# GpSimd's add of the diagonal's first tile, one step later

## The chip, the cores and the metric

The kernel runs on one core of one Trainium2 chip. The metric is the device time of one execution in microseconds (us). The kernel before takes 2315.55 us, the median of 3 runs (2315.52 to 2318.34).

The engines' names in the profile: PE is the matrix engine TensorE (PEld its weight loads), DVE is VectorE, ACT is ScalarE, POOL is GpSimd, SP is SyncE, which issues most of the transfers.

## What is computed

A transformer block with adaptive layer norm, in float32. x has 2 batches of 2048 tokens with 512 features; there are 16 heads of 32 features, and the MLP's hidden width is 2048:

```python
mod = silu(condition) @ Wada + bada
sh_a, sc_a, gt_a, sh_m, sc_m, gt_m = split(mod, 6, axis=1)
xm = layernorm(x, g1, be1) * (1 + sc_a) + sh_a
# attention(xm): q, k, v from xm @ Wqkv
scores = q k^T * hd**-0.5;  scores = where(causal, scores, -inf)
out = (softmax(scores) v) @ Wproj + bproj
x = x + gt_a * out
xm = layernorm(x, g2, be2) * (1 + sc_m) + sh_m
x = x + gt_m * (gelu(xm @ W1 + b1) @ W2 + b2)
```

## The kernel before

The work goes in phases: queries, keys and values of the first batch (with the weight preparation beside it), attention of the first batch, its output projection, the same three for the second batch, and then the two layers of the MLP for both batches. The change lies in the attention phase.

**Units and steps.** Attention of a batch is 16 units (c, i): a chunk c of four heads, and a block i of 512 queries (i from 0 to 3). The first chunk takes the blocks in the order 0, 1, 2, 3, the others in the order 0, 2, 1, 3. So units 3, 7, 11 and 15 have i = 3, and units 6, 10 and 14 have i = 1. A unit walks over the keys up to its queries in 4i + 3 steps (`steps_of`, line 696). The first 4i steps have one full tile of 128 keys each, all of it below the diagonal. The last three are the diagonal: step 4i has its first tile (d0 in what follows), step 4i + 1 has the second and the fourth tile packed together (d1), and step 4i + 2 the third (d2).

**What a step does.** `scores_t` (line 594) computes the transposed scores of the step's keys for four heads into PSUM (`st`: a product `fold` x `sel` that subtracts each row's maximum, and one of keys and queries). ScalarE writes the exponentials into the tile `e` (line 635), of which there are four slots (`E_BUFS`). On the diagonal GpSimd then sets what lies above it to zero with `affine_select` (line 643): one instruction for d0, two for d1, one for d2. Two steps later (`LAG`) TensorE multiplies the masked tile by the values into `o`.

**The softmax's sums.** For the full steps and for d0 the exponential tiles are added up before they are summed over the keys: the first two of a group of four tiles start a chain `ee` (`begin_chain`, line 664), the others are added (`add_to`, line 661, both through `add`, line 654). One add is a GpSimd instruction of 128 x 2048 elements (line 656). In the last unit of a batch it is four VectorE instructions of 128 x 512 (line 659). A product `sm<-ee` with a matrix of ones then sums the chain over its keys. d0's tile goes into the unit's last chain, whose product comes four steps after d0. d1 and d2 are summed by products of their own (`sm<-e`). There are two slots of `ee`.

**Scores ahead.** Between these products TensorE also computes scores of later units (`s`), whose row maxima VectorE takes (lines 495 and 500). How many are put into a step follows from costs (`due`, `weight`).

**What sets the order.** Matmuls, and the instructions that are wrapped in `act(...)`, keep the order in which the program issues them, each on its engine. This holds for the exponentials, the masks and the adds. A planner places the rest, transfers among them, by its own model of the time, so their order can change with a change elsewhere. GpSimd carries masks and adds in one stream, in program order.

**Around the end of the attention.** In the last unit `prepare` (line 446) multiplies the first attention outputs by the softmax's inverses on VectorE (line 467) and adds a bias row on GpSimd (line 465). `finish` (line 676) stores a unit's output and sums (lines 684 and 683). The output projection (`project_phase`, line 1209) loads the sums' last part (`r`, line 373), rows of x (`xt`, line 1225) and two attention outputs (`at`, line 1234), and multiplies `at` on GpSimd (line 1265) before TensorE multiplies it by the projection weights (`ps_o`). In the first batch weight pieces of the MLP are loaded in the same stretch (line 1153) into slots of `qst` and `vv`.

Of the kernel before, what the change touches and what calls it, by code (L numbers as in the profile page):

```python
# [27 lines left out]
def dit_block_kernel(  # L28
# [43 lines left out]
    TQ = QB // P  # L72
# [512 lines left out]
    def attention_phase(row):  # L585
        b, vv, kst, qst = row.b, row.vv, row.kst, row.qst
        with pool(f"att{b}") as ap, pool(
# [66 lines left out]
            def add(u, dst, x, y):  # L654
                if u < len(units) - 1:
                    act(nc.gpsimd.tensor_tensor(dst, x, y, ALU.add))  # L656
                    return
                for h in range(HC):
                    act(nc.vector.tensor_tensor(dst[:, h], x[:, h], y[:, h], ALU.add))

            def add_to(u, chain, es):
                add(u, chain, chain, es)

            def begin_chain(u, es0, es1):
                chain = ap.tile([P, HC, QB], F32, tag="ee", name="ee", bufs=EE_BUFS)
                add(u, chain, es0, es1)
                return chain

            def products(dst, lhs, es, q0, at, first, last):
                for h in range(HC):  # L670
                    mm(
                        dst[h * HD : (h + 1) * HD, q0:], lhs(h),
                        es[:, h, at : at + QB - q0], start=first, stop=last,
                    )

            def finish(u, o, sm):

                c, i = units[u]
                ot = ap.tile([P, QB], F32, tag="ot", name="ot", bufs=2)
                act(nc.scalar.copy(ot, o))  # L680
                sums = ap.tile([P, QB], F32, tag="sums", name="sums", bufs=2)
                act(nc.scalar.copy(sums, sm))
                nc.sync.dma_start(sums_d[b][u], sums[0:P:HD, :])
                nc.sync.dma_start(od[b][i][:, c, :], ot)
# [5 lines left out]
            def flush(upto):  # L690
                while pending and pending[0][0] <= upto:
                    pending.pop(0)[1]()
# [16 lines left out]
            def due(u, step):  # L709

                rate, past = 0.0, weight[step]
                for v in range(u + 1, len(units)):

                    left = sum(weight[step : max(step + 1, starts[v] - 3)])
                    rate = max(rate, (cum[v] - row.spent) / left)
                return row.spent + rate * past

            for u, (c, i) in enumerate(units):
                if NQ <= u + AHEAD < len(units):
                    row.load_queries(u + AHEAD)  # L720
                if u % NQ == 0 and c + 1 < C:
                    row.load_keys(c + 1, 0, NG)
                steps = len(steps_of[u])
                for n_step, tiles in enumerate(steps_of[u]):
                    last = n_step == steps - 1
                    if n_step == 0:
                        summed = set()
                        o = ps_op.tile([P, QB], F32, tag="o", name="o")
                        sm = ps_op.tile([P, QB], F32, tag="sm", name="sm")
                    ready = row.at  # L730

                    n = row.count(
                        due(u, starts[u] + n_step) - QB // 2,
                        u + AHEAD - (n_step < 2 and u > 0),
                    )
                    if u == 0 and n_step < LAG:

                        n = max(n, HC)
                    es, rest = scores_t(u, n_step, n)
                    rest = len(row.todo) - rest  # L740
                    make_rows = False
                    if u + 1 < len(units) and row.rows_made == u + 1:
                        if last:
                            row.score(row.count(cum[-1], u + 1))
                        make_rows = last or (ready > u + 1 and n_step >= 1)
                    row.inverses(u, n_step)
                    if u == len(units) - 1:
                        row.prepare(n_step)
                    if make_rows and not last:
                        row.rows(u + 1)  # L750
                    flush(now)
                    if make_rows and last:
                        row.rows(u + 1)
                    row.score(max(0, len(row.todo) - rest))

                    def tile_by_tile(dst, lhs, es, tiles, first, last):
                        at = 0
                        for n, (j, q) in enumerate(tiles):
                            products(
                                dst, lambda h: lhs(j, h), es, q, at,  # L760
                                first and n == 0, last and n == len(tiles) - 1,
                            )
                            at += QB - q

                    def values(es=es, tiles=tiles, c=c, o=o, first=n_step == 0, last=last):
                        tile_by_tile(
                            o,
                            lambda j, h: vv[:, j, (c * HC + h) * HD : (c * HC + h + 1) * HD],
                            es, tiles, first, last,
                        )  # L770

                    def row_sums(es, last, tiles=((0, 0),), sm=sm, summed=summed):
                        first = not summed
                        summed.add(len(summed))
                        tile_by_tile(sm, lambda j, h: ones[:, :HD], es, tiles, first, last)

                    pending.append((now + LAG, values))
                    sums_of, wait = None, 0
                    if n_step < i * TQ:
                        k = n_step % TQ  # L780
                        if k == 0:
                            even = es
                        elif k == 1:
                            chain = begin_chain(u, even, es)
                        else:
                            add_to(u, chain, es)
                        if k == TQ - 1 and n_step + 1 < i * TQ:
                            sums_of, wait = (chain, False), 2
                    elif i and n_step == i * TQ:
                        add_to(u, chain, es)  # L790
                        sums_of, wait = (chain, False), 2
                    else:

                        sums_of, wait = (es, last, tiles), i > 0 and not last
                    if sums_of:
                        pending.append(
                            (now + LAG + wait, lambda f=row_sums, s=sums_of: f(*s))
                        )
                    if last:
                        pending.append((now + LAG, lambda u=u, o=o, sm=sm: finish(u, o, sm)))  # L800
                    pending.sort(key=lambda p: p[0])
                    now += 1
# [471 lines left out]
    with pool("wada") as wp, pool("qkv0") as qp, pool("hl0") as hp, pool(  # L1274
# [161 lines left out]
        pieces.done()  # L1436

    attention_phase(row)


    past, row = row, Row(1)
    with pool("qkv1") as qp, pool("ps_qkv1", bufs=6, space=PSUM) as ps_mm:
# [29 lines left out]
        with pool("hl1") as hp:  # L1472
# [17 lines left out]
            pieces.done()  # L1490

    attention_phase(row)
    ps_s_cm.__exit__(None, None, None)

# [541 lines left out]
```

## Time and profile before

| what | us |
|---|---|
| median of 3 runs | 2315.55 |
| the profiled execution | 2314.76 |
| its span, first to last instruction | 2313.0 |
| TensorE busy in the span | 2252.9 (97%) |
| GpSimd busy in the span | 1021.5 (44%) |
| ScalarE busy in the span | 1006.2 (44%) |
| attention, first batch | from about 212 to 736 |
| attention, second batch | from about 973 to 1494 |
| one GpSimd add (line 656), mean | 4.58 |
| one GpSimd mask (line 643), median | 0.637 |

A row of the timeline is: start in us, length in us, engine, line, operation, the tile written and the tiles read, the shape, how many instructions are merged, and in brackets how long the engine was idle before it and what ended that wait. A row of the waits is: who waited, for whom, the sum in us, how often, the longest. A row by stretch has the window, its length, the busy time and count of each engine, then TensorE's granted clock (1.00 is full speed), the share of the transfer engines and GB/s. Idle time of an engine that is not the bottleneck costs nothing.

### The profile page before, as it was taken

What the parts mean: (1) busy time and instruction counts of PE and PEld (TensorE: products, weight loads), DVE (VectorE), ACT (ScalarE), POOL (GpSimd) and SP (SyncE); (2) the same over time, 40 slices, a digit from 0 to 9 for tenths busy, and PEclk for the clock granted to TensorE, in tenths of its full rate; (3) what the DMA queues carried; (4) which work ended last, traced back from release to release, by engine and by line L of the source; (5) the groups of instructions that cost most, each with busy time, mean ns of one, the idle gap of its engine ahead of it and who ended that gap; (6) DMA issues with size and microseconds to landing.
All of it is one profiled execution on the core that took longest, in us unless ns stands there. A gap on an engine that the chain in (4) does not pass through costs nothing.

```text
span 2313.0 us, 32545 instructions
## 1 busy us (share of the span) xinstructions
PE 2252.9 (97%) x12033; PEld 1374.5 (59%) x12033; DVE 1443.8 (62%) x3025; ACT 1006.2 (44%) x1952; POOL 1021.5 (44%) x561
## 2 busy tenths in 40 slices
PE   7999999999999999999999999999999999999998
PEld 5777555555544588755555554344684585486477
DVE  4677766767757667777577766662573483375366
ACT  4434555555555244355555556513313322332320
POOL 7252986877782692278777879340000000000000
PEclk9999999999999999999999999999999999999999
DMA  9877143231323796523223123272354253353433
GB/s 302 279 259 195 37 92 69 65 83 47 99 94 128 258 300 230 162 67 78 71 72 88 47 74 114 98 254 86 118 165 150 99 174 130 116 171 121 153 113 131
DMA packets 160505, 311.52 MB, mean 135 GB/s; under 512 B 16545, under 2 KB 48845, under 8 KB 158553
## 3 DMA queue, kind: packets, MB, share of 16 engines
q1 hardware_dynamic: 155488, 285.53, 40.9%
q0 software_dynamic: 4480, 23.36, 2.6%
q8 instruction: 95, 1.56, 0.3%
q14 instruction: 66, 0.53, 0.1%
q10 hardware_dynamic: 376, 0.55, 0.1%
HBM read 229.95 MB, written 87.29 MB: 137 GB/s over the span
## 4 chain that ended last, share of the span: by engine, by line
PE 84%; POOL 6%; DVE 5%; issue 2%; ACT 1%; DMA 1%; SPq 0%; POOLq 0%; DVEq 0%; ACTq 0%
PE ps_a L206 24%; PE st L206 16%; PE ps_b L206 12%; PE o L206 9%; PE s L206 8%; PE ps_c L206 6%; POOL ee L656 4%; PE sm L206 4%; PE ps_o L206 2%; DVE junk L495 2%; PE ps_xt L214 1%; DVE mx L500 1%; ACT e L635 1%; PE ps_o L214 1%; POOL e L643 0%
## 5 line engine op out<-in xcount | busy, mean ns | idle before, releaser
L635 ACT ACTIVATE e<-st 128x512 f32<-128x512 f32 (+1 forms) x1152 | 571.5, 578 | 392.9 <-PE st L206 370.6
L500 DVE TENSOR_REDUCE mx<-s 128x1 f32<-128x512 f32 x578 | 381.6, 686 | 223.0 <-PE s L206 221.9
L656 POOL TENSOR_TENSOR ee<-ee,e 128x2048 f32<-128x2048 f32 x106 | 485.8, 4583 | 16.3 <-ACT e L635 9.0
L206 PE MATMUL st<-qst,kst 128*128 128x512 f32 (+3 forms) x1280 | 412.4, 388 | 0.0
L206 PE MATMUL s<-kst,qst 128*128 128x512 f32 (+3 forms) x1054 | 381.2, 393 | 10.7 <-DVE mx L500 6.1
L206 PE MATMUL ps_a<-sum,w 128*128 128x256 f32 (+1 forms) x1088 | 346.6, 454 | 0.0
L206 PE MATMUL o<-e,vv 128*32 128x512 f32 (+3 forms) x2560 | 293.7, 540 | 9.4 <-POOL e L643 9.3
L206 PEld LDWEIGHTS st<-qst,kst 128*128 128x128 f32 x1280 | 230.0, 189 | 100.6 <-issue 67.6
L206 PEld LDWEIGHTS ps_a<-sum,w 128*128 128x128 f32 x1088 | 206.3, 190 | 109.8 <-issue 91.4
L495 DVE CUSTOM_DVE_ANT_0 junk<-s,causal 128x128 bf16<-128x128 f32 (+3 forms) x476 | 224.9, 472 | 65.0 <-PE s L206 51.3
L656 POOL TENSOR_TENSOR ee<-e 128x2048 f32<-128x2048 f32 x42 | 192.5, 4583 | 138.9 <-ACT e L635 130.8
L206 PEld LDWEIGHTS s<-kst,qst 128*128 128x128 f32 x1054 | 196.0, 188 | 70.5 <-DVE mx L500 21.7
L1615 DVE TENSOR_TENSOR h<-c,ps_b 128x512 f32<-128x512 f32 x32 | 22.0, 688 | 202.4 <-PE ps_b L206 202.4
L206 PEld LDWEIGHTS <-sel 32*128 32x128 bf16 x1152 | 29.4, 91 | 196.2 <-issue 196.2
L500 DVE TENSOR_REDUCE mx<-st 128x1 f32<-128x512 f32 x190 | 129.6, 682 | 0.4
L643 POOL TENSOR_SCALAR_AFFINE_SELECT e<-e 128x512 f32<-128x512 f32 x128 | 82.1, 663 | 91.8 <-ACT e L635 89.6
L1789 ACT ACTIVATE h<-h,cols 128x512 f32<-128x512 f32 x96 | 69.3, 722 | 120.4 <-DVE h L1615 120.4
L206 PE MATMUL ps_b<-sum,w 128*128 128x256 f32 (+1 forms) x384 | 120.6, 450 | 0.0
L206 PE MATMUL st<-fold,sel 32*128 32x512 bf16 (+1 forms) x1152 | 117.5, 374 | 2.8 <-DVE mx L495 1.7
L206 PEld LDWEIGHTS o<-e,vv 128*32 128x32 f32 x2560 | 57.8, 109 | 96.2 <-issue 64.3
L984 POOL TENSOR_TENSOR lo<-lo,hi 128x512 fp32r<-128x512 f32 x32 | 40.8, 1276 | 132.4 <-ACT hi L982 130.7
L206 PEld LDWEIGHTS ps_b<-sum,w 128*128 128x128 f32 x384 | 73.0, 190 | 37.2 <-issue 30.6
(206 smaller groups left out, 3094.7 us busy)
## 6 DMA issues: line engine op xcount, KB each, us to landing
kst<-k SPq DMA_DIRECT2D x128, 256.0 KB
qst<-q SPq DMA_DIRECT2D x128, 256.0 KB
w<-w1d SPq DMA_DIRECT2D x32, 896.0 KB
w<-w2d SPq DMA_DIRECT2D x28, 1024.0 KB
w<-w2d SPq DMA_DIRECT2D x28, 768.0 KB
q<-hi SPq DMA_DIRECT2D x32, 256.0 KB
q<-lo SPq DMA_DIRECT2D x32, 256.0 KB
k<-hi SPq DMA_DIRECT2D x32, 256.0 KB
```

The costliest lines, as they stand in the source:

```text
L206: return tc.keep_in_program_order(nc.tensor.matmul(*args, **kw))
L214: return tc.keep_in_program_order(nc.tensor.transpose(dst, src, ident[:n, :n]))
L495: nc.vector.tensor_tensor_reduce(junk[:, :w], x, causal[:, QB - w :], 1.0, MASKED, ALU.add, ALU.max, m,)
L500: nc.vector.tensor_reduce(m, x, axis=AX.X, op=ALU.max)
L635: act(nc.scalar.activation(e4[:, h, :w], sts[h][:, :w], AF.Exp))
L643: nc.gpsimd.affine_select(d, d, pattern=[[0, HC], [1, P]], compare_op=ALU.is_ge, fill=0.0, base=0, channel_multiplier=-1,)
L656: act(nc.gpsimd.tensor_tensor(dst, x, y, ALU.add))
L984: engine.tensor_tensor(lo, d, hi.bitcast(F32), ALU.subtract)
L1615: act(nc.vector.tensor_tensor(dst, x, y, ALU.add))
L1789: nc.scalar.activation(d, ps, AF.Gelu, bias=col(r_b1 + half * HF + f, 1))
```

## The change

In units with i > 0 the add of d0's tile to the chain is not issued in d0's step any more. The tile is kept under the name `single`, and the add is issued in the next step, after `scores_t` has issued the exponentials and the two masks of d1. The step at which the product `sm<-ee` is issued stays the same. Units with i = 0 have no chain and are untouched. In the last unit of each batch the same move holds for VectorE's four adds.

```diff
                     pending.append((now + LAG, values))
                     sums_of, wait = None, 0
+                    if i and n_step == i * TQ + 1:
+                        add_to(u, chain, single)
                     if n_step < i * TQ:
                         k = n_step % TQ
                         if k == 0:
...
                         if k == TQ - 1 and n_step + 1 < i * TQ:
                             sums_of, wait = (chain, False), 2
                     elif i and n_step == i * TQ:
-                        add_to(u, chain, es)
+                        single = es
                         sums_of, wait = (chain, False), 2
                     else:
```

## The prediction

> **What bounds the kernel now.** I read the page's busy line first, then the table by stretch of the span, then the list of waits with TensorE as the waiter, and last the order of time around each wait.
>
> ```profile
> span 2313.0 us, 32545 instructions
> PE 2252.9 (97%) x12033; PEld 1374.5 (59%) x12033; DVE 1443.8 (62%) x3025; ACT 1006.2 (44%) x1952; POOL 1021.5 (44%) x561
> ...
> 212.00:736.00 524.00, 513.04 (x3661) 264.64 (x3661) 364.49 (x886) 302.36 (x608) 385.04 (x142) 0.99 0.31 78
> ...
> 973.00:1494.00 521.00, 510.29 (x3661) 263.29 (x3660) 364.54 (x886) 302.39 (x608) 385.20 (x142) 1.00 0.30 78
> 1494.00:1560.00 66.00, 66.00 (x185) 31.55 (x184) 40.36 (x73) 9.22 (x15) 30.43 (x25) 1.00 0.75 254
> ...
> PE o L206 <- POOL e L643: 9.3, 8, 2.4
> ```
>
> TensorE is the bound: busy 97%. The stretches 212 to 736 and 973 to 1494 are the two attention phases. In them TensorE stands idle about 11 us each, and the only wait on GpSimd there is the value product `o` waiting for a causal mask: 9.3 us in 8 waits. The changed line touches exactly these masks. GpSimd works in order, so the 4.6 us add of the first diagonal tile (d0) stands in front of the masks of the second diagonal step (d1). A unit with much work behind shows the chain (GpSimd, ScalarE and TensorE in order of time, unit 14 of the first batch):
>
> ```profile
> 682.08 0.63 POOL L643 TENSOR_SCALAR_AFFINE_SELECT e<-e 128x512 f32<-128x512 f32 x1
> 682.80 4.56 POOL L656 TENSOR_TENSOR ee<-ee,e 128x2048 f32<-128x2048 f32 x1
> 687.29 1.84 POOL L643 TENSOR_SCALAR_AFFINE_SELECT e<-e 128x512 f32<-128x512 f32 x3
> ...
> 680.07 2.06 ACT L635 ACTIVATE e<-st 128x512 f32<-128x512 f32 x4 [0.95 <-PE st L206]
> ...
> 688.00 1.93 PE L206 MATMUL o<-e,vv 128*32 128x384 f32 x16 [2.43 <-POOL e L643]
> 692.42 1.94 PE L206 MATMUL sm<-ee,ones 128*32 128x512 f32 x8
> 696.12 0.40 PE L206 MATMUL st<-fold,sel 32*128 32x512 bf16 x4
> ...
> 688.00:694.00 6.00, 6.00 (x32) 2.27 (x36) 2.04 (x4) 2.07 (x4) 1.12 (x2) 0.50 0.01 2
> ```
>
> The exponentials of d1 end at 682.13, but their masks start at 687.29, when the add is through, and the product of d1 waits 2.43 us. The last line is a stretch (TensorE, weight loads, DVE, ACT, POOL busy, then the granted clock): right behind the wait the clock is 0.50. So a wait is paid twice here, once as idle time and once as slow matmuls. The other units with such a wait:
>
> ```profile
> 345.92 1.64 PE L206 MATMUL o<-e,vv 128*32 128x384 f32 x16 [1.90 <-POOL e L643]
> 350.15 1.06 PE L206 MATMUL sm<-ee,ones 128*32 128x512 f32 x8
> ...
> 1106.75 1.07 PE L206 MATMUL o<-e,vv 128*32 128x384 f32 x16 [1.63 <-POOL e L643]
> 1109.44 1.06 PE L206 MATMUL sm<-ee,ones 128*32 128x512 f32 x8
> ...
> 1443.64 1.20 PE L206 MATMUL st<-qst,kst 128*128 128x512 f32 x4
> 1447.27 1.07 PE L206 MATMUL o<-e,vv 128*32 128x384 f32 x16 [2.43 <-POOL e L643]
> 1448.28 0.39 PE L206 MATMUL st<-fold,sel 32*128 32x512 bf16 x4
> 1454.03 0.39 PE L206 MATMUL st<-fold,sel 32*128 32x512 bf16 x4
> ```
>
> **The change part by part.** No instruction is added or removed. 22 GpSimd adds (11 units of each batch) go from in front of the two masks of d1 to behind them; in the last unit of each batch the four VectorE adds go behind one multiplication of line 467. In the order in which the changed kernel is built, TensorE and ScalarE keep their order exactly.
>
> *The idle time removed.* Four waits: 1.90 + 2.43 + 1.63 + 2.43 = 8.4 us. (What is left of the 9.3 lies in the two last units, whose adds are VectorE's; it stays.) In unit 14 the masks of d1 can start at 682.7, when the mask of d0 ends, and are done at 684.0, 1.6 us ahead of the product's turn at 685.57 (688.00 - 2.43).
>
> *The slow clock removed.* The two units 3 do the same matmuls from `o` to `sm`: 350.15 - 345.92 = 4.23 us against 1109.44 - 1106.75 = 2.69, so the slow clock cost the first 1.54. In unit 14 of the first batch 6.0 us ran at 0.50, so 3.0 us were lost. From `o` to the second next `st<-fold` it took 696.12 - 688.00 = 8.12 us there and 1454.03 - 1447.27 = 6.76 in the second batch: the second lost 3.0 - 1.36 = 1.6. Sum 1.5 + 3.0 + 1.6 = 6.1 us, if without the wait the clock stays up.
> A rule bears on this. The Trainium skill, "TensorE: Matmul & The Clock Gate", section "Why this matters for your kernels", says that throughput falls in mid-kernel when TensorE idles longer than about 3 us between bursts. By it gaps of 1.90 and 2.43 us would leave the clock alone, the slow stretches would have another cause and stay, and the sum would lose these 6.1 us. The trace does not agree (0.50 right behind the 2.43 us wait, and full speed behind the 1.63 us one), so I take the rows.
>
> *What the later add makes late.* Its readers are the row-sum product `sm<-ee`, the slot of `e` that the exponential four steps on wants, and the mask of the third diagonal step (d2) behind it. In unit 14 the add would run from 684.0 to 688.6 (4.56). TensorE, no longer held, reaches `sm<-ee` after `o` (1.01 = 1448.28 - 1447.27), the `st<-fold` group (0.39) and four `st` (1.20), the last two overlapping 0.07 each: 685.57 + 2.46 = 688.0. A new wait of 0.6 us, twice: 1.2 us. The mask of d2 then ends at 689.2, ahead of its product. In units without a backlog GpSimd idles until the exponentials of d1 are there, the worst case for the add's end:
>
> ```profile
> 284.07 4.58 POOL L656 TENSOR_TENSOR ee<-ee,e 128x2048 f32<-128x2048 f32 x1
> 283.73 2.07 ACT L635 ACTIVATE e<-st 128x512 f32<-128x512 f32 x4 [1.73 <-PE st L206]
> 294.00 2.06 ACT L635 ACTIVATE e<-st 128x512 f32<-128x512 f32 x4 [1.40 <-PE st L206]
> 295.65 1.06 PE L206 MATMUL sm<-ee,ones 128*32 128x512 f32 x8
> ```
>
> There the add starts at 285.80 + 1.3 (two masks) = 287.1 and ends at 291.7, before the slot is wanted (294.00) and the sum is read (295.65). It costs nothing as long as these 2.3 us of cover last. The VectorE adds of the last units end within about half a us of where they did, under a wait of `o` for a mask that exists already: nothing.
>
> *SyncE's queue, which the planner reorders.* At the end of the first batch the built order puts three of the four `qst` weight loads (line 1153 before) ahead of the stores of `ot` and `sums`, and three `vv` weight loads ahead of the load of `r`. Before:
>
> ```profile
> 735.96 0.32 SPq L684 DMA_DIRECT2D o<-ot  x1
> 736.44 0.52 SPq L683 DMA_DIRECT2D sum<-sums  x1
> 741.11 1.92 SPq L1153 DMA_DIRECT2D qst<-in_L_cond_W_dram  x4
> 743.12 0.41 SPq L373 DMA_DIRECT2D r<-sum  x1
> ...
> 746.42 0.43 SPq L1234 DMA_DIRECT2D at<-o  x1
> ...
> SPq L1153 <- POOL kst L1265: 4.1, 1, 4.1
> ...
> 755.14 1.27 POOL L1265 TENSOR_TENSOR at<-at,qst 128x512 f32<-128x512 f32 x1 [7.17 <-DMA at<-o]
> 765.50 1.27 POOL L1265 TENSOR_TENSOR at<-at,qst 128x512 f32<-128x512 f32 x1
> ...
> 735.56 20.87 PE L206 MATMUL ps_o<-kst 128*128 128x512 f32 x48
> ...
> 764.01 3.94 PE L206 MATMUL ps_o<-kst,at 128*128 128x512 f32 x8
> ...
> 768.66 24.20 PE L206 MATMUL ps_o<-kst,at 128*128 128x512 f32 x56
> ...
> DMA packets 3660, 7.58 MB, mean 303 GB/s; under 512 B 602, under 2 KB 1626, under 8 KB 3276
> ...
> qst<-in_L_cond_W_dram SPq DMA_DIRECT2D x4, 128.0 KB
> ```
>
> SyncE is held at the `qst` loads until 741.11, for GpSimd's multiplications of line 1265 (the wait of 4.1 us). After the change both stores and three more loads are issued behind that point: 0.48 + 0.52 + 3 x 0.48 = 2.4 us more before `at` is issued at 746.42. By data it is the same: 256 KB of `ot` and 3 x 128 KB more ahead of `at` at 303 GB/s is 2.1 us. `at` landed at 755.1 and its last part was multiplied at 766.77; TensorE wanted it one pair before the end of its first eight (764.01 + 6 x 20.87 / 48 = 766.6). So there is no cover: TensorE waits 2.4 us more, a gap as long as those of unit 14, so I add one slow stretch of 1.6 us (as in unit 14 of the second batch). Bounds: nothing (the load comes no later, because transfers overlap) and 2.4 + 3.0 = 5.4 us. I take 4.0, nearest to the rows of unit 14. In the second batch only stores and weight loads trade places, and TensorE is busy without a gap from 1494 to 1560; I take nothing.
>
> *Sum.* -8.4 - 6.1 + 1.2 + 4.0 = -9.3 us. The profiled execution took 2314.76 us (span 2313.0), so 2305.5; the median of the runs is 0.8 above it. I predict 2306 us.
>
> **The rivals.**
> - The stores and loads at the batch's end are hidden after all: -13.3 us, 2302. For it: transfers overlap, and the issue of `x` loads behind also gets easier. Against it: the load of `at` is waited for 7.17 us by GpSimd already.
> - The slow clock is not the waits' doing (the skill's rule above gives this too, by itself): -8.4 + 1.2 + 2.4 = -4.8, 2311. Against it: in the attention I find the clock low only right behind such waits.
> - The wait only moves: the row sums or the slot of `e` hold TensorE as long as the masks did. This needs the add to end about 2 us later than worked out in the units with a backlog. Then 8.4 is paid elsewhere and 4.0 is added: about 2315 to 2319.
> - Slower, by one thing: the late `at`. If TensorE comes out of that wait slow and stays slow, the output projection, 24.2 us of work behind 768.66, drags. It decides once more than 13.3 - 2.4 = 10.9 us of that work run at 0.50; all of it would give 13 us more than before, 2329. Against it: the slow stretches above lost 1.5 to 3.0 us each and ended by themselves.
>
> **How the numbers follow.** Likeliest (2306) 0.57, hidden at the batch's end 0.22, clock independent 0.08, wait moves 0.08, projection drags 0.05. A measurement here tells about 0.2% (4.6 us) from no change, so faster means under 2310.9. The likeliest and the hidden case lie there almost wholly, of the third half: faster 0.81; the third's other half and much of the fourth within 0.2%: 0.11; slower 0.08. The range goes from 2300 (hidden, and the new 1.2 us waits gone too) to 2312 (the clock case and a transition at its upper bound).
>
> **What would show it.** The waits of `o` on the mask should be gone except in the last units (under 1 us in all). The granted clock should be 1.0 through both attention phases, with no 0.50 stretch behind units 3 and 14. `sm<-ee` should wait on line 656's add for about 0.6 us in the two units 14. SyncE should issue `at` about 2.4 us later after the last product of the first batch, and TensorE show a gap of some 3 us in the first `ps_o<-kst,at` group, perhaps a 0.50 clock behind it. I am wrong if other diagonal steps show new waits, or if the clock falls in the attention without a wait before it.

## The result and the profile after

The changed kernel takes 2307.71 us, the median of 7 runs (2305.5 to 2309.61). The kernel before, run on the same chip, takes 2315.52 us (7 runs, 2310.09 to 2319.1). The ratio is 0.9966, with a 95% interval from 0.9952 to 0.998: 7.8 us less. The profiled execution is the fastest of the seven, 2305.5 us with a span of 2303.7, against 2314.76 and 2313.0 before.

Of the kernel after, the first two lines of the page (span; busy time of each engine, share and instructions):

```profile
span 2303.7 us, 32538 instructions
...
PE 2250.5 (98%) x12033; PEld 1374.2 (60%) x12033; DVE 1439.6 (62%) x3025; ACT 1006.1 (44%) x1952; POOL 1021.1 (44%) x561
```

The work is the same. TensorE is busy 2.4 us less (2252.9 to 2250.5) and idle 6.9 us less (60.1 to 53.2): a part of the gain are matmuls that ran faster. The two profiles also differ in a slow stretch outside the attention: in the kernel after the clock is 0.50 from 890.28 to 893.69 us, behind a wait of 2.52 us ahead of the second batch's attention, and in the kernel before it is 1.00 behind the same wait. Of the kernel after, TensorE's waits (waiter, whom it waited for, sum, how often, longest):

```profile
PE sm L206 <- DVE ee L659: 1.3, 2, 0.6
PE ps_o L206 <- POOL at L1267: 1.1, 1, 1.1
...
PE sm L206 <- POOL ee L656: 0.8, 2, 0.4
...
PE o L206 <- POOL e L643: 0.2, 1, 0.2
```

The wait of `o` on the masks has shrunk from 9.3 us in 8 to 0.2 us. In its place stand the two predicted waits of the row sums on the add (0.8 us), one at the batch's end (1.1 us), and one of the last units, `sm` on VectorE's adds (1.3 us), which I had not predicted. Of the kernel after, GpSimd, TensorE and the stretch behind in unit 14 of the first batch (rows as those of the unit in the prediction):

```profile
679.16 1.81 POOL L643 TENSOR_SCALAR_AFFINE_SELECT e<-e 128x512 f32<-128x512 f32 x3
680.93 4.56 POOL L656 TENSOR_TENSOR ee<-ee,e 128x2048 f32<-128x2048 f32 x1
685.45 0.64 POOL L643 TENSOR_SCALAR_AFFINE_SELECT e<-e 128x512 f32<-128x512 f32 x1
...
682.61 1.07 PE L206 MATMUL o<-e,vv 128*32 128x384 f32 x16
...
685.55 1.07 PE L206 MATMUL sm<-ee,ones 128*32 128x512 f32 x8 [0.42 <-POOL ee L656]
...
685.50:691.00 5.50, 5.45 (x60) 2.19 (x60) 3.67 (x6) 4.94 (x10) 0.58 (x1) 1.00 0.14 51
```

The three masks of d0 and d1 now run as one group (x3) ahead of the add and end at 680.97. The product of d1 starts at 682.61 without a wait, and takes 1.07 us where it took 1.93. The sum waits 0.42 us for the add, and the clock behind is 1.00.

To see where the time went I measured each unit from its first `o` product to that of the next one (for the last unit: to the first `ps_o`; for the projection: from there to the first `ps_a`). Units that are not in the table agree within 0.1 us, but for unit 6 of the second batch (+0.34).

| stretch (us) | before | after | difference |
|---|---|---|---|
| unit 3, batch 1 / 2 | 53.70 / 52.14 | 50.80 / 51.06 | -2.91 / -1.08 |
| unit 13, batch 1 / 2 | 39.21 / 39.24 | 39.10 / 39.10 | -0.11 / -0.14 |
| unit 14, batch 1 / 2 | 25.70 / 24.31 | 20.75 / 20.75 | -4.95 / -3.56 |
| unit 15, batch 1 / 2 | 37.99 / 37.99 | 39.20 / 39.19 | +1.21 / +1.20 |
| projection, batch 1 | 57.13 | 58.13 | +1.00 |

Units 3, 13 and 14 gain 12.8 us, and the last units and the projection give 3.4 back. That leaves -9.3; the small rest (+0.1) makes it the -9.26 between the two profiled executions.

### The profile page after: what moved, and what is told of

Same layout as the page of the kernel before. It is cut to its first block, busy times and chain, and to the rows that moved or that the text cites. A ratio compares the mean times of both kernels' runs of the same rounds, so it can differ in the third digit from the quotient of the medians.

```text
span 2303.7 us, 32538 instructions
## 1 busy us (share of the span) xinstructions
PE 2250.5 (98%) x12033; PEld 1374.2 (60%) x12033; DVE 1439.6 (62%) x3025; ACT 1006.1 (44%) x1952; POOL 1021.1 (44%) x561
```

## The experiments

Two questions stood open. Where do the 3.4 us given back come from? And is the slow clock really the waits' doing? Every kernel below computes the whole block. Differences are against runs of the kernel before on the same chip; `units` in the diffs has 16 entries, so `len(units) - 1` is the last unit, whose adds are VectorE's.

**GpSimd's adds alone** (`pool_only`). The add moves in all units but the last.

```diff
+                    if i and n_step == i * TQ + 1 and u < len(units) - 1:
+                        add_to(u, chain, single)
...
-                        add_to(u, chain, es)
+                        single = es
+                        if not (u < len(units) - 1):
+                            add_to(u, chain, es)
```

> The add moves in the units whose adds are GpSimd's; the last unit of each batch keeps VectorE's adds where they were, and SyncE's order is then the one of before. My theory: the change's gain is all in units 3 and 14 (wait plus slow clock, -2.9, -1.1, -5.0 and -3.6 us by the trace of the change), and the last unit's part only costs (1.2 us in each batch, and 1.0 in the first projection). So this is faster than the change by about 3.4 us: ratio to before about 0.995, some 2304 us; the stretch from the first o of unit 15 to the first ps_o back at 38.0 us (39.2 with the change), the first projection back at 57.1 (58.1). Rival: the last unit's part helps or does nothing, and the time is the change's, ratio 0.9966.

Measured: 2303.47 us (2299.59 to 2309.51), ratio 0.9941 (0.9928 to 0.9955). SyncE's queue has the order of before. Unit 14 takes 20.76 us in both batches, the last units 37.97, the projection 57.09. The expectation held.

**The last unit's adds alone** (`last_only`). The same edit with `u == len(units) - 1` in both places.

> Only the last unit of each batch moves its VectorE adds (SyncE's order is then the changed one); all GpSimd adds stay. My theory: slower than before by 2 x 1.2 + 1.0 = 3.4 us, ratio about 1.0015, unit 15 to ps_o 39.2 us, first projection 58.1, and the waits of o on the mask in units 3 and 14 unchanged. Rival (the last unit's part is free, as I predicted, and the batch's end costs 4.0): 38.0 and 61, ratio 1.0017. Second rival: it gains, ratio under 1.

Measured: 2321.26 us (2314.26 to 2326.37), ratio 1.0018 (1.0006 to 1.003). The waits of the masks are back, the last units take 39.20 and 39.19 us, and SyncE's queue has the changed kernel's order. The projection takes 57.68 us, half a us more than before and not one.

So the two halves of the change come apart. All of the gain belongs to GpSimd's adds. The late batch end belongs to VectorE's: the planner reorders SyncE's queue only where those move. The longer unit 6 of the second batch belongs to VectorE's too: it is 0.32 to 0.35 us longer in the three executions where they move, because TensorE waits 0.78 us there for row maxima of line 495 instead of 0.42, and 0.06 to 0.07 us shorter in the two executions of GpSimd's half. Why that wait grows stays open. Of the three kernels, VectorE's adds of d0 and GpSimd's work beside them in unit 15 of the first batch. Before:

```profile
727.88 4.45 DVE L659 TENSOR_TENSOR ee<-ee,e 128x512 f32<-128x512 f32 x4 [0.53 <-POOL e L643]
...
727.01 0.84 POOL L643 TENSOR_SCALAR_AFFINE_SELECT e<-e 128x512 f32<-128x512 f32 x1 [17.16 <-ACT e L635]
727.82 1.28 POOL L465 TENSOR_TENSOR kst<-kst,bgate 128x512 f32<-128x512 f32 x1
729.59 2.20 POOL L643 TENSOR_SCALAR_AFFINE_SELECT e<-e 128x512 f32<-128x512 f32 x2 [0.49 <-ACT e L635]
731.75 1.71 POOL L465 TENSOR_TENSOR kst<-kst,bgate 128x512 f32<-128x512 f32 x1
```

After, with TensorE's wait for those adds:

```profile
718.85 1.28 DVE L467 TENSOR_TENSOR kst<-kst,qst 128x512 f32<-128x512 f32 x2
720.66 5.51 DVE L659 TENSOR_TENSOR ee<-ee,e 128x512 f32<-128x512 f32 x4 [0.53 <-POOL e L643]
...
719.19 1.44 POOL L643 TENSOR_SCALAR_AFFINE_SELECT e<-e 128x512 f32<-128x512 f32 x1 [17.17 <-ACT e L635]
720.60 1.27 POOL L465 TENSOR_TENSOR kst<-kst,bgate 128x512 f32<-128x512 f32 x1
721.83 2.12 POOL L643 TENSOR_SCALAR_AFFINE_SELECT e<-e 128x512 f32<-128x512 f32 x2
723.93 1.70 POOL L465 TENSOR_TENSOR kst<-kst,bgate 128x512 f32<-128x512 f32 x1
...
726.23 0.62 PE L206 MATMUL sm<-ee,ones 128*32 128x512 f32 x1 [0.63 <-DVE ee L659]
```

With the last unit's adds alone:

```profile
729.47 5.52 DVE L659 TENSOR_TENSOR ee<-ee,e 128x512 f32<-128x512 f32 x4 [0.53 <-POOL e L643]
```

Each time VectorE waits 0.53 us for the mask. But after the change the multiplication of line 467 goes ahead of the adds, so it runs at the same time as the mask, and the mask takes 1.44 us instead of 0.84. That makes GpSimd's stream later by as much, so that the masks of d1 no longer wait for the exponentials. Before, the first of them starts at 729.59, 0.02 us behind VectorE's second add (729.57); that add takes 0.68 us, as it does alone. After, it starts at 721.83, 0.52 us ahead of the second add (722.35), which takes 1.11 us. The fourth add then falls on GpSimd's next add of line 465 and takes 1.75 us instead of 1.11. So the four take 5.51 us instead of 4.45. `sm` has to wait for them, and `sm` closes the unit.

**A quarter of the add behind the masks** (`quarter`). In GpSimd's units three of the four heads are added in the old place and the fourth in the new one. That leaves three quarters of an add in front of the masks, and so a shorter wait.

```diff
+                    if 0 < i and u < len(units) - 1 and n_step == i * TQ + 1:
+                        add(u, chain[:, 3:], chain[:, 3:], single[:, 3:])
...
-                        add_to(u, chain, es)
+                        single = es
+                        if u < len(units) - 1:
+                            add(u, chain[:, :3], chain[:, :3], es[:, :3])
+                        else:
+                            add_to(u, chain, es)
```

> In the GpSimd units three of the four heads of d0 are added ahead of the masks of d1 and one head behind them, so the wait becomes shorter by a quarter of 4.58 us, 1.1 us, but does not vanish: 1.3 us in the units 14, 0.5 to 0.8 in the units 3. My theory (the clock falls because of the wait, and not for a gap as short as 1.63 us): no 0.50 stretch in the attention, and so more than half of the gain for a quarter of the add: about -9 us, ratio 0.996. Rival (the slow clock comes independently of the wait): slow stretches stay behind units 3 and 14, gain 4 x 1.1 = -4.5 us, ratio 0.998.

Measured: 2305.08 us (2304.22 to 2306.16), ratio 0.9952 (0.9939 to 0.9966). Of this kernel, the row of the waits, the longest of them in the timeline, and the two stretches behind the waits of the units 14:

```profile
PE o L206 <- POOL e L643: 4.9, 8, 1.3
...
686.08 1.07 PE L206 MATMUL o<-e,vv 128*32 128x384 f32 x16 [1.31 <-POOL e L643]
...
686.10:692.70 6.60, 6.60 (x72) 3.05 (x72) 2.50 (x4) 3.81 (x9) 2.34 (x3) 1.00 0.11 41
1440.30:1447.00 6.70, 6.66 (x76) 3.10 (x77) 2.50 (x4) 3.91 (x9) 2.40 (x3) 1.00 0.17 59
```

About half of the idle time still stands (4.9 of 9.3 us; in the four units of the prediction 4.0 of 8.4), but the clock no longer falls, and most of the gain is there: the units 3, 13 and 14 gain 10.5 us, against 12.8 in GpSimd's half. A wait of 1.3 us costs itself; three of the four longer ones of the kernel before cost more than themselves.

**Waits of chosen length** (`dose_a`, `dose_b`). On the kernel before, the first mask of d1 is repeated in units 5, 7, 9 and 11, which had no wait. A repeated mask changes no value; it only keeps GpSimd busy.

```diff
+                        again = {5: 4, 7: 5, 9: 5, 11: 6}.get(u, 0) if len(tiles) > 1 and n_t == 0 else 0
+                        for _ in range(1 + again):
```

The second kernel has `{5: 3, 7: 4, 9: 3, 11: 3}`. Each was timed once.

> The kernel before, with the first mask of d1 repeated (it changes nothing in the data) 4, 5, 5 and 6 times in units 5, 7, 9 and 11, which have no wait before. One repeat is 0.6 us, less the 1.0 to 1.4 us by which the first mask was early: waits of o of about 1.3, 1.6, 1.85 and 2.6 us, in both batches. My theory: behind the 2.6 us waits the granted clock is 0.50 for 3.4 us or 6.8 us, behind the 1.3 us waits it stays 1.00, between them either can be, as the wait falls into one window of the clock's gate or across two. Each slow stretch makes its unit 1.6 to 3 us longer beyond its wait. Rival: no slow stretch at the new waits.

> As dose_a with fewer repeats of the mask: 3, 4, 3 and 3 in units 5, 7, 9 and 11. By the waits that dose_a showed (1.75 us for 4 repeats in unit 5, 2.4 for 5 in unit 9, 3.25 for 6 in unit 11) the waits of o should be 1.1 us in unit 5, 1.6 in unit 7, 1.2 in unit 9 and 1.4 in unit 11, in both batches. My theory: at 1.1 to 1.4 us the granted clock stays 1.00 and the units are longer by the wait alone; 1.6 us can go either way. Rival: any wait of TensorE brings the slow stretch at times; then units 5, 9 and 11 show some, 1.5 us each.

Measured: 2339.22 and 2322.87 us. The waits of `dose_a` came out longer than expected: 1.67, 2.10, 2.39 and 3.16 us in the first batch. Behind waits of 0.95 to 1.45 us (`dose_b`) the clock stayed up in all eight, and each unit grew by about its wait. Behind 1.66 to 3.16 us (`dose_a`) it fell in five of eight. The expectation that it would fall behind each of the longest waits failed: the same wait did both. Of `dose_a`, unit 11 of the first batch and of the second, and the stretches behind:

```profile
626.88 1.94 PE L206 MATMUL o<-e,vv 128*32 128x384 f32 x16 [3.16 <-POOL e L645]
...
1398.87 1.07 PE L206 MATMUL o<-e,vv 128*32 128x384 f32 x16 [3.16 <-POOL e L645]
...
626.90:632.80 5.90, 5.90 (x37) 3.33 (x41) 0.82 (x1) 2.12 (x4) 2.09 (x4) 0.50 0.01 3
1398.90:1404.80 5.90, 5.90 (x75) 3.25 (x76) 0.82 (x1) 2.88 (x6) 2.90 (x5) 1.00 0.01 3
```

At 0.50 TensorE does 37 matmuls in 5.90 us, at 1.00 it does 75. The unit grew by 5.93 us the first time, and by 3.25 the second.

What tells the two apart is where the wait falls. The granted clock in the trace changes only at multiples of 3.413 us from one another. I cut each wait at these instants, in the five traces (before, `last_only`, `quarter` and the two `dose` kernels) with 34 waits of `o` on a mask of over 0.9 us, 14 of them followed by 0.50. Of the two 3.16 us waits the first is cut into 2.30 and 0.85, the second into 1.72 and 1.44. Wherever the larger part was 1.85 us or more, 0.50 followed from the end of its step on, for one or two of these steps (what decides between one and two, these traces do not show); where it was 1.63 us or less, it never did. Between 1.64 and 1.72 both occurred. Outside the attention one wait of 2.52 us stands in all ten traces (`ps_xt` on ScalarE, between 886 and 908 us), and 0.50 followed in seven. In two of the seven the larger part was only 1.63 and 1.53 us, but there other gaps of TensorE bring the idle time of the step to 2.00 and 1.91 us. So it seems to be the idle time of the whole step that counts, and not that of one wait. The Trainium skill, "TensorE: Matmul & The Clock Gate", section "What's actually happening", says that the activity is judged in a window of 3413 ns which runs freely and does not start with the kernel: the trace agrees with its step of 3.413 us. That section's table puts the half clock behind at least one idle window; if that means a window that is idle throughout, the trace does not bear it out: 1.85 us in one was enough.

So one wait has several prices. The 2.4 us of unit 14 cost, by execution, nothing more than themselves (the unit takes 22.75 us, first batch of `dose_b`), one slow step (24.2 to 24.3) or two (25.6 to 25.7), against 20.75 after the change, which has the sum's wait of 0.42 in it. That adds to the spread of the kernel before (9.0 us over its 7 runs, against 4.1 after), but by how much is not shown, and it isn't the only thing that does: GpSimd's half alone, without these waits, spread over 9.9 and 8.0 us. The ten traces show two other stretches that vary. The first batch's first `o` product comes between 220.5 and 226.5 us (latest in `pool_only`, whose profiled execution is the slowest of its five), and the second batch's queries, keys and values take 187.2 to 190.6 us.

**The moved add in two halves** (`halves`). `pool_only`, with the add as two GpSimd instructions of two heads, to let the first heads' sums start while the rest is added.

```diff
-                        add_to(u, chain, single)
+                        for k in (0, 2):
+                            h = slice(k, k + 2)
+                            add(u, chain[:, h], chain[:, h], single[:, h])
```

> As pool_only, but the moved add is two GpSimd instructions of two heads each. The row sums of the first two heads then wait for the first half alone. My theory: in the units 14 the wait of sm<-ee on the add (0.42 us with the change) goes, because its first half ends 2.3 us earlier, and unit 14 to unit 15 takes 20.3 to 20.4 us in place of 20.75; nothing else moves by more than 0.1 us; against pool_only -0.8 us, too little to be seen in the medians, ratio to before about 0.994. Rival: the second half, which ends later by the cost of one more instruction, is waited for as long, and unit 14 stays at 20.75 or grows.

Measured: 2304.22 us (2302.79 to 2309.12), ratio 0.996 (0.9946 to 0.9974). Of this kernel, GpSimd in unit 14:

```profile
682.07 4.72 POOL L656 TENSOR_TENSOR ee<-ee,e 128x1024 f32<-128x1024 f32 x2
686.73 0.65 POOL L643 TENSOR_SCALAR_AFFINE_SELECT e<-e 128x512 f32<-128x512 f32 x1
```

The expectation failed: the unit takes 20.88 us in both batches, not less than 20.75. The first heads' products do start 0.5 us earlier, but the products of the four heads run side by side on TensorE, so the group ends with the last head, and the two halves together take 4.72 us instead of 4.56.

**The whole change and GpSimd's half, side by side** (`after_again`, `pool_only_again`). Unchanged copies, timed on one chip in the same rounds.

> The changed kernel once more, timed on the same chip as the next run. By the traces the change is -12.8 us in units 3, 13 and 14 and +2.4 in the two last units, and about +0.5 to +1 in the first projection: ratio to before 0.996.

> The GpSimd part alone beside the whole change. My theory: 2.4 to 3.4 us faster than after_again, some 2304 against 2307 us, ratio to before 0.9945 to 0.995. Rival: equal times, so that the last unit's part would not matter to the total. In the unit-by-unit times the last units take 38.0 us here and 39.2 there, each.

Measured: 2306.96 us (2306.19 to 2308.09), ratio 0.9961 (0.9949 to 0.9973), for the whole change, and 2305.54 us (2301.24 to 2309.28), ratio 0.9953 (0.994 to 0.9966), for GpSimd's half. The medians stand in the expected order, but 1.4 us apart with intervals that overlap; the times alone do not separate them. The profile says why the gap is small. In this execution of GpSimd's half the last unit took 38.64 us, not 37.97, although nothing was moved in it. Of `pool_only_again`, VectorE's adds there and GpSimd beside them:

```profile
721.33 5.56 DVE L659 TENSOR_TENSOR ee<-ee,e 128x512 f32<-128x512 f32 x4 [0.53 <-POOL e L643]
...
722.99 1.67 POOL L643 TENSOR_SCALAR_AFFINE_SELECT e<-e 128x512 f32<-128x512 f32 x2 [0.44 <-ACT e L635]
724.63 1.71 POOL L465 TENSOR_TENSOR kst<-kst,bgate 128x512 f32<-128x512 f32 x1
```

They took 5.56 us with the multiplication behind them, as before. Here the first mask of d1 (722.99) started 0.03 us ahead of the second add (723.02): the mask took 0.64 us and the add 1.14, and the fourth add again fell on line 465. So how long these adds take beside GpSimd varies from one execution to the next. In the old order the mask and the second add start within 0.04 us of each other in all seven profiled executions. In five the add kept its 0.68 us and the last units took 38.0; in two (this one and `dose_b`) the mask kept its 0.64, and they took 38.64. In the new order the mask is half a us ahead, and all three executions show 39.2. Of the 1.2 us that the last unit lost, only some 0.55 (39.19 - 38.64) are there even against the slower outcome of the old order. The first projection took 59.33 us in this execution of the whole change, 2.2 more than before where 0.5 to 1 was expected. The old order of SyncE's queue gave 56.8 to 57.6 in seven profiled executions, the new one 57.7, 58.1 and 59.3 in three.

## Why the prediction was right

The forecast was 2306 us, and the median is 2307.71, a ratio of 0.9966. The sum was -9.3 us and the profiled execution shows -9.26. But two of its terms were wrong by about as much in opposite directions. And the -9.26 compares a profile of the kernel before that lies near its median with the fastest of seven executions after: the medians are 7.8 us apart, so the agreement to a tenth is luck.

- **The four waits and the slow clock behind two of the units 14 and a unit 3, -8.4 - 6.1 + 1.2 = -13.3:** measured -12.8, in the same profile of the kernel before from which the terms were read. The waits are gone, and the clock is 1.00 there. The sum's new wait is 0.42 us each and not 0.6. Each unit 3 gave some 0.5 us back: the wait had covered another one. Of the kernel after, TensorE in unit 3 of the first batch:

```profile
344.17 1.07 PE L206 MATMUL o<-e,vv 128*32 128x384 f32 x16
345.18 0.96 PE L206 MATMUL st<-fold,sel 32*128 32x512 bf16 x4
```

  Right behind `o` the group `st<-fold` takes 0.96 us, where it takes 0.40 in unit 14. The row shows no wait, only length: three of its products start at 345.18 to 345.27 and the last at 345.76, just behind the end of ScalarE's exponentials at 345.71. From that I take it that it waits for ScalarE to free the scores' PSUM; no run tried that.
- **The clock as the waits' doing:** right. `quarter` left shorter waits and full clock, and in the `dose` kernels the clock fell where nothing had been changed but the wait. By the rival that the clock falls for other reasons, `quarter` would have kept the 0.50 stretches. What the step did not say is that the price is drawn anew in each execution: the 6.1 us belong to the one profile that I had, and other executions pay from nothing to two slow steps for the same wait.
- **The batch's end, +4.0:** the right place, too large; measured +1.0 in this execution. SyncE did issue `at` later: 12.5 us after the first `ps_o` (741.41 - 728.93) instead of 10.9. That is 1.6 us and not 2.4. Of the kernel after, SyncE and TensorE there:

```profile
733.27 1.41 SPq L1155 DMA_DIRECT2D qst<-in_L_cond_W_dram  x3
734.73 0.47 SPq L684 DMA_DIRECT2D o<-ot  x1
...
736.41 1.39 SPq L1155 DMA_DIRECT2D vv<-in_L_cond_W_dram  x3
...
741.41 0.46 SPq L1236 DMA_DIRECT2D at<-o  x1
...
728.93 20.87 PE L206 MATMUL ps_o<-kst 128*128 128x512 f32 x48
...
757.38 2.74 PE L206 MATMUL ps_o<-kst,at 128*128 128x512 f32 x6
761.19 1.13 PE L206 MATMUL ps_o<-kst,at 128*128 128x512 f32 x2 [1.07 <-POOL at L1267]
```

  The gap came where it was predicted, behind six products of the first `ps_o<-kst,at` group, but it was 1.07 us long, and the clock stayed up: the 1.6 us of slow matmuls in this term did not happen. In `last_only` and `after_again`, with the same order, `at` is issued 12.7 and 13.4 us after the first `ps_o`, and the gap is 0.63 and 2.28 us. So the predicted delay of 2.4 us was about reached once, and the clock stayed up even then (that gap is cut into 1.50 and 0.78). The rival that all of it is hidden does not hold either: executions of this order show +0.5 to +2.2 against the 57.13 of before.
- **The last units' adds, "nothing":** this is the step that failed, +2.4 us. I moved four adds by half a us and kept their length of 4.45 us. They took 5.51: the multiplication that went ahead of them meets GpSimd's mask, the mask they wait for takes 0.6 us longer, and what GpSimd does next then falls on the second and the fourth add. The wait of `sm` on line 659 was not in the prediction at all. `last_only` shows it without the rest of the change; `pool_only_again` and `dose_b` show that some 0.65 us of the 1.2 can come in the old order too. So the step was wrong in taking the adds' length as fixed while GpSimd works beside them.
- **The other moved adds, "nothing":** right. Their units agree with before within 0.1 us; the +0.34 of unit 6 of the second batch comes with VectorE's adds. The cover of 2.3 us held.
- **The wait moves; the projection drags:** neither. TensorE's new waits on the add are 0.8 us in all, and the projection's clock stayed at 1.00. ScalarE's exponentials do wait longer for GpSimd's adds and masks (29.9 us in all instead of 20.8), but no further wait of TensorE comes of it.

The two wrong terms give back 3.4 us where the prediction had 4.0. That the total came out is in this part luck; that the four waits and their slow clock were the gain is not.

## What to carry to other kernels

Price a wait of the bounding engine by the clock behind it as well as by its length: here waits under about 1.6 us cost themselves, and longer ones anything from themselves to two and a half times as much (5.3 us for a wait of 2.1 in `dose_a`), so that shortening a wait by a half can bring most of what removing it would. Ask of an edit that does one thing in two places what each place brings: here GpSimd's half carried the gain, and VectorE's half, included only because the same line serves both, moved a shared queue and lengthened its neighbours. Before a term is taken from one profile, look whether its row could come out differently in another execution of the same kernel.

## What the hardware showed that was not expected

- The clock follows idle time as it falls into fixed steps of 3.413 us: 1.85 us or more in one step was always followed by 0.50, and 3.16 us cut into 1.72 and 1.44 was not.
- VectorE's additions and GpSimd's masks and adds slow each other down when they run together, by amounts that change from run to run: the same four adds took 2.49 us a few steps earlier in the unit, and 4.45, 5.51, 5.52 and 5.56 beside GpSimd's work; a mask of 0.64 us took 0.82 to 1.48. Which of two gives way can hang on hundredths of a us: of a mask and an add that started within 0.04 us of each other, one took its own 0.64 or 0.68 us and the other 1.14 to 1.19. Of the kernel after, the earlier four:

```profile
716.44 2.49 DVE L659 TENSOR_TENSOR ee<-ee,e 128x512 f32<-128x512 f32 x4
```

  The Trainium skill, "GPSIMD Engine Reference", section "1. Specifications", says that GpSimd shares its SBUF interfaces with VectorE and contends with instructions of VectorE that have two SBUF inputs. These adds are such instructions, and the rows agree.
